# Softmax weights of a graph attention layer transposed through memory, with row sums from a 129th column

## The chip, the cores and the metric

The kernel runs on one core of a Trainium2 chip. The metric is device microseconds of that core for one execution, as the median of several runs. Engines are named as in the profile: PE (matmul) with PEld (its weight loads), DVE (vector), ACT (scalar, activations), POOL (GpSimd), SP (which issues most DMAs). Everything is float32.

## The reference

64 graphs of 256 nodes with 128 features go through four layers, each of the form x = x + layer(relu(layernorm(x))). The layers share one 256x256 adjacency matrix. What matters here is layer 0, an additive attention:

```python
W1, W2 = (W[:, :F], W[:, F:])                 # W is adj
s1 = jnp.einsum('bkf,ef->bke', x, W1)
s2 = jnp.einsum('bkf,ef->bke', x, W2)
pre = s1[:, :, None, :] + s2[:, None, :, :] + b_lin
h = jnp.where(pre >= 0, pre, ALPHA * pre)
e = jnp.einsum('bije,e->bij', h, a) + bias     # bias is adj
attn = jax.nn.softmax(e, axis=2)
out = jax.nn.sigmoid(jnp.einsum('bij,bjf->bif', attn, x))
```

For every pair of nodes of a graph 256 values are made, rectified and summed with weights: that is nearly all of the work. Layer 1 is a second message-passing layer, layer 2 a masked dot-product attention, layer 3 a gated recurrent unit of five steps.

## The kernel before

**Groups and order.** The 64 graphs go in 34 groups: two of one graph, thirty of two, two of one (`GROUPS`, line 15). No scheduler orders the instructions: the kernel writes them out in the order that a planner of its own (the loop from line 1359) finds, which keeps a clock for each engine (`Model`, line 42) with a cost for each operation, and always emits the piece of work that can start first. Pieces come from generators: `head` and `senders` prepare a graph's attention, `Pairs` makes and multiplies the pair values, `softmax0` finishes layer 0, and `layer1`, `layer2`, `layer3` or `layer3_across` follow. A `yield "pe"` in a generator names the engine that the next piece needs; a condition and an earliest time may stand behind it. Each chain of pieces has a pace (line 1322 on).

**The pairs.** A row t of a graph stands for eight tiles of 128x256 for each half (ec) of the 256 values. Three engines make such tiles: ACT (line 720, a Relu with a bias), POOL (line 725) and DVE (line 702, four or eight tiles at once). PE then sums them over the partitions with a sliding weight `a_win` (line 786); a batch is four matmuls over 512 columns (ec 0) or eight over 256 (ec 1). When at least five batches wait for PE (`SPARE`), the planner merges: DVE adds half of one batch on top of another (line 744), which costs DVE eight instructions for two rows and saves PE one batch of 256-column matmuls. So the planner trades work between DVE and PE. All `r` tiles come from 12 buffers, which PE frees.

**The end of layer 0** (`softmax0`, line 791). DVE adds the mask and takes each row's maximum (line 800); ACT takes the exponential and has its sum accumulated (line 809, an ACTIVATE and an ACTIVATION_READ_ACCUMULATOR for each half); DVE inverts the sums (line 815). PE transposes the four 128x128 blocks of weights into the PSUM bank of `e_ps` (lines 821 and 135), ACT copies them to SBUF with a factor of 0.5 (line 826), PE multiplies them with `h` (lines 832 and 128), ACT takes the tanh scaled by the inverse sums (line 839), and DVE adds the result to x (line 841).

**Transposes through memory** (`crossed`, line 97). Elsewhere 128x128 blocks are transposed by two DMAs on SP: one stores the tile to HBM (`there`, line 101), the next reads it back with its axes swapped (line 103). Both are issued one after the other, so SP waits at the read until the store has landed. The planner takes a time for the pair from a clock of its own for the memory (`TURN`, `SURE`) and lets the reader start no sooner. Groups 0 to 31 (`BY_MEMORY`) do this ahead of layers 1 and 2, groups 0 to 27 (`BY_MEMORY_3`) ahead of layer 3 and after four of its five steps.

**Layout.** h and its transpose in layer 0 are kept block by block: `h` as [128, G, 128], `h_t` as [128, G, 128], where G is the number of 128-node blocks of the group (2 or 4). In the later layers they are interleaved, [128, 128, G], so that a read of a crossing takes G neighbouring floats.

**The last two groups** and, for layer 3, groups 28 to 33 use PE transposes (`by_pe`). In `layer3` a group holds the shared PSUM banks for all five steps (`inside`, line 1262).

Of the kernel before, what the change touches and what calls it, by code (L numbers as in the profile page):

```python
# [24 lines left out]
TURN = 12500  # L25
# [16 lines left out]
class Model:  # L42
# [16 lines left out]
    def transfer(self, e):  # L59

        self.memory = max(self.memory, self.t[e] + 900) + TURN
        return self.memory + SURE
# [3 lines left out]
def kernel(ctx: ExitStack, tc: tile.TileContext, ins: dict, out: bass.AP):  # L66
# [30 lines left out]
    def crossed(src, tag, name, by, bufs=1):  # L97

        shape = [P, src.shape[1], src.shape[2]]
        there = dp.tile(shape, F32, tag="there%d" % src.shape[2], name="there", bufs=3)  # L100
        nc.sync.dma_start(out=there, in_=src)
        t = bp.tile(shape, F32, tag=tag, name=name, bufs=bufs)
        nc.sync.dma_start(out=t, in_=there.rearrange("p f g -> f p g"))
        return t, model.transfer(by)
# [67 lines left out]
    adj_n = fetch([P, 2, N], "adj_n", adj.rearrange("(c p) m -> p c m", p=P), nc.scalar)  # L172
# [66 lines left out]
    def constants0():  # L239
# [125 lines left out]
        dve(1).tensor_copy(left_b, p[:, P + 1 : P + 2])  # L365
        counts["left"] += 1
# [81 lines left out]
    def ln_relu(space, xt, tag, ln, when=None, at=None, across=False):  # L448
# [22 lines left out]
        for g in range(G):  # L471
            if g % 2 == 0:
                yield "act"
            if g == 0:
                shape = [P, P, G] if across else [P, G, P]
                h = space.tile(shape, F32, tag=ln, name=tag, bufs={ap: 3, bp: 1}.get(space))
            act(P, 2, 1).activation(  # L477
                h[:, :, g] if across else h[:, g, :], xt[:, g, :], AF.Relu, bias=shift[:, g : g + 1],
                scale=rstd[:, g : g + 1],
            )  # L480
        return h

    def transpose_blocks(space, src, name, banks, when=None, tag=None, bufs=None):

        yield "pe", when
        G, _, W = sizes(src)
        tp = banks([P, G, P], name + "_ps")
        turn()
        for g in range(G):
            tr(tp[:, g, :], src[:, g, :])  # L490
        yield "act"
        t = space.tile([P, G, P], F32, tag=tag or name, name=name, bufs=bufs)
        act(W).copy(t, tp)  # L493
        return t


    def first_head(xt, to, snd):
# [3 lines left out]
        h_t = yield from transpose_blocks(ap, h, "h0t", psum_h)  # L501
# [26 lines left out]
    def head(xt, to):  # L528
        G, _, W = sizes(xt)
        h = yield from ln_relu(ap, xt, "h0", "h0")  # L530
        h_t = yield from transpose_blocks(ap, h, "h0t", psum_h, settled)
        to.update(h=h, h_t=h_t)
        if counts["left"] > 0:
            yield from bounds(to)
# [17 lines left out]
    def bounds(of):  # L552
# [4 lines left out]
        G = h_t.shape[1]  # L557
        p = psum_h([P, P], "bound_ps")
        model.op("pe", P * 1.676)
        for c in range(G):  # L560
            nc.tensor.matmul(
                p[bass.ts(c, 32), :], lhsT=left_w, rhs=h_t[:, c, :], start=True, stop=True
            )
# [13 lines left out]
    def senders(b, of, to):  # L577

        h_t = flat(of["h_t"][:, 2 * b : 2 * b + 2, :])
        if "bound" not in of:  # L580
# [3 lines left out]
        mm(p, lhsT=left2, rhs=h_t, start=True, stop=True)  # L584
# [3 lines left out]
            adj_l, p, of["bound"][:, 2 * b : 2 * b + 1], adj_n[:, 0, :], ALU.min, ALU.add  # L588
# [6 lines left out]
        for ec in range(2):  # L595
            mm(p[:, ec, :], lhsT=w_p[:, 1, bass.ts(ec, P)], rhs=h_t, start=True, stop=True)
# [5 lines left out]
    class Pairs:  # L602
# [5 lines left out]
        def __init__(self, g, b, of, snd):  # L608
# [8 lines left out]
            self.s1n_v = of["s1n"][:, :, bass.ts(b, N)].rearrange(  # L617
                "p c (k g t) -> p c g k t", k=2, g=4
            )
            self.s1n_b = of["s1n"][:, :, bass.ts(b, N)].rearrange(  # L620
                "p c (k g t) -> p c k g t", k=2, g=4
            )
# [49 lines left out]

        def nodes(self, batch, g2):
# [3 lines left out]
                (g, k, self.b * N + 32 * g + t + (P + k if two else k * P))  # L677
# [3 lines left out]
        def make(self, who):  # L681
# [10 lines left out]
            if who == "dve":  # L692
# [4 lines left out]
                if batch["two"]:  # L697
                    s1n = self.s1n_b[:, ec, 1, 2 * g2 : 2 * g2 + n, t : t + 2].unsqueeze(3)
# [51 lines left out]
        def open(self):  # L750
            b = self.b
            self.e_ps = ps_e.tile([P, 2, N], F32, tag="e", name="e_ps")
            for ic in range(2):
                mm(
                    self.e_ps[:, ic, :], lhsT=v2_rep,
                    rhs=flat(self.of["h_t"][:, 2 * b : 2 * b + 2, :]),
# [34 lines left out]
    def softmax0(g, b, of, e_ps, snd):  # L791
# [3 lines left out]
        for ic in range(2):  # L795
            yield "dve", lambda: "adj_l" in snd

            if ic == 0:
                nmax = sp.tile([P, 2], F32, tag="nmax", name="nmax")
            dve(N, more=10).tensor_tensor_reduce(  # L800
                e_ps[:, ic, :], e_ps[:, ic, :], adj_n[:, 1, :] if ic else snd["adj_l"], -1.0, FLT_MAX,
                ALU.add, ALU.min, nmax[:, ic : ic + 1],
            )
        for ic in range(2):
            yield "act"
            if ic == 0:
                pm = ap.tile([P, 2, N], F32, tag="pm", name="pm", bufs=1)
                rs = sp.tile([P, 2], F32, tag="rs", name="rs")
            act(N, 1, more=119).activation(  # L809
                pm[:, ic, :], e_ps[:, ic, :], AF.Exp, bias=nmax[:, ic : ic + 1], scale=-1.0,  # L810
                accum_out=rs[:, ic : ic + 1],
            )
        yield "dve"
        rh = sp.tile([P, 2], F32, tag="rh", name="rh")
        dve(2).reciprocal(rh, rs)
        yield "pe"
        pt_ps = e_ps
        turn()
        for jc in range(2):
            for ic in range(2):  # L820
                tr(
                    pt_ps[:, jc, bass.ts(ic, P)], pm[:, ic, bass.ts(jc, P)]
                )
        yield "act"
        pt = ap.tile([P, 2, N], F32, tag="pt", name="pt", bufs=1)
        act(2 * N, table=1).activation(pt, pt_ps, AF.Copy, scale=0.5)
        yield "pe"
        o_ps = e_ps[:, :, 0:P]
        for ic in range(2):
            for jc in range(2):  # L830
                mm(
                    o_ps[:, ic, :], lhsT=pt[:, jc, bass.ts(ic, P)], rhs=h[:, b * 2 + jc, :],
                    start=(jc == 0), stop=(jc == 1),
                )
        for ic in range(2):
# [38 lines left out]

    def by_pe(h, tag, bufs=None, when=None, space=bp):

        yield "pe", when
        if when:
            using_a.append(tag)
        G = h.shape[2]  # L880
        tp = psum_a([P, P, G], "h_t_ps")
        turn()
        for g in range(G):
            tr(tp[:, :, g], h[:, :, g])
        yield "act"
        t = space.tile([P, P, G], F32, tag=tag, name="h_t", bufs=bufs)
        act(P * G).copy(t, tp)
        return t
# [94 lines left out]
    def layer2(x2, by_memory):  # L983
        G, NB, W = sizes(x2)
        h = yield from ln_relu(bp, x2, "h2", "h", across=True)
# [57 lines left out]
    class Home:  # L1043
# [10 lines left out]

        def bank(self, shape, name):
# [12 lines left out]
    def layer3(x3, h3, h_t, home):  # L1068
# [7 lines left out]
        for step in range(STEPS):  # L1076
            yield "pe"
# [64 lines left out]
        yield "pe"  # L1142
# [5 lines left out]
        dve(W).tensor_tensor(x3, tp.rearrange("p (g n) -> p g n", g=G), x3, ALU.add)  # L1148

    def layer3_across(x3, lane):  # L1150
# [7 lines left out]
        hn = yield from ln_relu(bp, x3, "h3" + tag, "hn" + tag, across=True)  # L1158
# [57 lines left out]
    def first_norm(g, xt):  # L1216
        h = yield from ln_relu(bp, xt, "h1", "ln", across=True)
# [4 lines left out]

    def free_a():
        return not using_a
# [5 lines left out]
    def second_rest(g, xt):  # L1230
# [6 lines left out]
        if g >= len(GROUPS) - 2:  # L1237
            hn = yield from ln_relu(rp, xt, "h3", "r", no_tiles, across=True)
            h_t = yield from by_pe(hn, "r", None, free_a, rp)
        else:  # L1240
            hn = yield from ln_relu(
                bp, xt, "h3", "hn" + tag, lambda: done3(g - 2), across=True
# [12 lines left out]
    def last_rest(g, xt, hn=None, h_t=None, home=None):  # L1255
        if home is None:
            yield from layer3_across(xt, g % 2)
        else:
            if home.banks:
                yield "pe", lambda: n == len(graphs) and not (making or doing or multiplying)  # L1260
            else:
                yield "pe", lambda: not inside
                inside.append(g % 2)
            yield from layer3(xt, hn, h_t, home)
            if not home.banks:
                inside.remove(g % 2)
# [6 lines left out]
    class Chain:  # L1273
# [14 lines left out]
        def advance(self):  # L1288

            while self.queue:  # L1290
# [8 lines left out]
                self.due = max(self.due, self.earliest)  # L1299
# [3 lines left out]
        def start(self, paced):  # L1303

            if self.engine is None or (self.when and not self.when()):
                return None
            return max(
# [16 lines left out]
    lanes = [Chain(2300), Chain(2300)]  # L1324
# [5 lines left out]
    to_load = []  # L1330
# [28 lines left out]
    while True:  # L1359
# [17 lines left out]
        for e in ("pe", "dve", "act", "pool"):  # L1377
# [28 lines left out]
            if making and (freed or not making[0].fresh()):  # L1406
                at = max(model.t[e], freed[0] if making[0].fresh() else 0.0)
                if best is None or at < best[0]:
                    best = (at, e, None)
        if best is None:  # L1410
# [61 lines left out]
```

## Time and profile before

| | us |
|---|---|
| median of three runs | 4956.28 |
| lowest and highest of them | 4955.85, 4961.90 |
| the profiled execution | 4962.75 |
| its span, first to last instruction | 4960.9 |
| first matmul of line 786 starts | 16.4 |
| last matmul of line 786 starts | 4865.7 |

The granted TensorE clock was 0.999 over the span. A busy time in the profile is the union of an engine's instruction spans. ACT's instructions overlap in its pipeline: a tile of line 720 lasts 1212 ns by the group row and the next one ends about 365 ns later. So the cost of an instruction is taken from the spacing of neighbours in the timeline, not from the mean length in the group rows. In timeline rows of PE an `xN` counts two records for a matmul instruction, except for transposes, which have one.

SP's rows are issues. DMA queue q1 carries every crossing; 204 of them are in the profile.

### The profile page before, as it was taken

To read this page: it belongs to the slowest core of one execution; us is meant where nothing else is said; L and a number is where in the kernel's file an instruction comes from. 1 tells how busy PE (TensorE), PEld (TensorE's weight loads), DVE (VectorE), ACT (ScalarE), POOL (GpSimd) and SP (SyncE) were. 2 spreads that over 40 slices of the span, in tenths; PEclk is the share of its full clock that TensorE was granted. 3 is DMA by queue.
4 is the path that set the end of the run, shared out by engine and by line. 5 is a ranking of instruction groups with operands and counts; after the bars stand their busy time and mean duration, and the time that the engine had idled before them with its cause. 6 is when DMAs were issued, how large, how long until landed. Compare 5 with 4: busy or idle time off the path is not lost.

```text
span 4960.9 us, 176723 instructions
## 1 busy us (share of the span) xinstructions
PE 4923.5 (99%) x69735; PEld 2389.7 (48%) x69735; DVE 4841.8 (98%) x8229; ACT 4873.2 (98%) x12812; POOL 4756.8 (96%) x10545
## 2 busy tenths in 40 slices
PE   9999999999999999999999999999999999999998
PEld 4454545554454544444445444444454444444444
DVE  9999999999999999999999999999999999999994
ACT  8999999999999999999999999999999999999994
POOL 8999999999999999999999999999999999999981
PEclk9999999999999999999999999999999999999999
DMA  0357576777676776866757656656666555542310
GB/s 21 10 17 23 25 30 27 32 32 30 30 33 27 32 32 28 34 27 30 33 27 30 30 27 32 32 26 32 30 32 32 26 31 30 29 26 12 19 9 8
DMA packets 3431090, 132.92 MB, mean 27 GB/s; under 512 B 3369201, under 2 KB 3405937, under 8 KB 3430257
## 3 DMA queue, kind: packets, MB, share of 16 engines
q1 hardware_dynamic: 3429712, 121.35, 56.5%
q8 instruction: 547, 8.96, 0.9%
q14 instruction: 287, 2.34, 0.3%
q10 hardware_dynamic: 544, 0.26, 0.0%
HBM read 61.48 MB, written 60.10 MB: 25 GB/s over the span
## 4 chain that ended last, share of the span: by engine, by line
PE 85%; ACT 7%; DVE 5%; POOL 1%; issue 1%; DMA 0%; ACTq 0%; DVEq 0%; POOLq 0%
PE e_ps L786 53%; PE gate_ps L128 8%; PE hv_ps L128 5%; ACT r L720 5%; PE m_ps L128 5%; PE s_ps L128 3%; DVE r L702 3%; PE o_ps L128 2%; PE e_ps L128 2%; PE rc_ps L128 1%; POOL r L725 1%; PE rsum_ps L128 1%; DVE r L744 1%; PE e_ps L135 1%; PE th_ps L128 1%
## 5 line engine op out<-in xcount | busy, mean ns | idle before, releaser
L725 POOL TENSOR_SCALAR r<-s,s1n 128x256 f32<-128x256 f32 x9920 | 4509.6, 543 | 47.1 <-PE e_ps L786 21.1
L720 ACT ACTIVATE r<-s_act,s 128x256 f32<-128x256 f32 x9768 | 4421.0, 1212 | 1.1 <-PE e_ps L786 1.0
L786 PE MATMUL e_ps<-r,a_win 128*32 128x256 f32 (+1 forms) x41040 | 3323.2, 464 | 9.1 <-DVE r L702 7.5
L702 DVE TENSOR_TENSOR r<-s_ps,s1n 128x2048 f32<-128x2048 f32 (+1 forms) x1367 | 2417.3, 1804 | 0.0
L786 PEld LDWEIGHTS e_ps<-r,a_win 128*32 128x32 f32 x41040 | 1394.2, 110 | 1603.7 <-issue 825.0
L744 DVE SCALAR_TENSOR_TENSOR r<-s_ps,s1n,r 128x256 f32<-128x256 f32 x4056 | 1671.5, 472 | 0.8 <-POOL r L725 0.3
L477 ACT ACTIVATE h<-xt,bsh,brs 128x128 f32<-128x128 f32 x512 | 417.6, 1318 | 7.5 <-POOL bsh L470 7.5
L720 ACT ACTIVATE r<-s,s 128x256 f32<-128x256 f32 x512 | 319.2, 1416 | 0.0
L128 PE MATMUL m_ps<-adj_q,hn 128*32 128x256 f32 x4096 | 252.1, 380 | 1.6 <-ACT hn L1140 1.6
L128 PEld LDWEIGHTS m_ps<-adj_q,hn 128*32 128x32 f32 x4096 | 160.8, 132 | 89.4 <-issue 25.4
L1192 ACT ACTIVATE gate_ps<-gate_ps,bz 128x512 f32<-128x512 f32 (+1 forms) x140 | 202.5, 1447 | 0.0
L1194 ACT ACTIVATE hv_ps<-hv_ps,bh 128x512 f32<-128x512 f32 (+1 forms) x140 | 200.9, 1435 | 0.0
L1180 ACT ACTIVATE m_ps<-gate_ps,br 128x512 f32<-128x512 f32 (+1 forms) x140 | 194.0, 1386 | 0.0
L1176 ACT COPY m_t<-m_ps 128x512 f32<-128x512 f32 (+1 forms) x140 | 184.7, 1319 | 0.0
L128 PE MATMUL gate_ps<-m_t,t_w_w 128*32 128x512 f32 (+1 forms) x1360 | 174.8, 568 | 0.4 <-ACT m_t L1090 0.3
L128 PE MATMUL hv_ps<-rh,u_th 128*32 128x512 f32 (+1 forms) x1360 | 170.9, 567 | 1.3 <-DVE rh L1103 1.3
L128 PE MATMUL gate_ps<-m_t,w_t 128*32 128x512 f32 (+1 forms) x1360 | 171.1, 568 | 0.6 <-ACT m_ps L1100 0.6
L128 PE MATMUL hv_ps<-m_t,t_w_w 128*32 128x512 f32 (+1 forms) x1360 | 171.0, 567 | 0.0
L809 ACT ACTIVATE pm<-e_ps,nmax 128x256 f32<-128x256 f32 x128 | 145.7, 1138 | 2.4 <-DVE nmax L800 2.4
L128 PE MATMUL gate_ps<-hf,u_t 128*32 128x512 f32 (+1 forms) x1088 | 139.8, 567 | 0.0
L128 PE MATMUL s_ps<-h0t,w_p 128*32 128x256 f32 (+1 forms) x1568 | 138.9, 445 | 0.6 <-ACT h0t L493 0.5
L940 ACT ACTIVATE th_ps<-th_ps,a_src 128x256 f32<-128x256 f32 x128 | 134.8, 1053 | 1.5 <-PE th_ps L128 1.5
(223 smaller groups left out, 4612.8 us busy)
## 6 DMA issues: line engine op xcount, KB each, us to landing
there<-hf SPq DMA_DIRECT2D x104, 256.0 KB
hn<-there SPq DMA_DIRECT2D x104, 256.0 KB
there<-h SPq DMA_DIRECT2D x86, 256.0 KB
h_t<-there SPq DMA_DIRECT2D x60, 256.0 KB
xt<-in_x_dram SPq DMA_DIRECT2D x30, 256.0 KB
out_dram<-xt SPq DMA_DIRECT2D x30, 256.0 KB
h3t<-there SPq DMA_DIRECT2D x26, 256.0 KB
row<-rows SPq DMA_DIRECT2D x128, 0.5 KB
```

The costliest lines, as they stand in the source:

```text
L128: nc.tensor.matmul(out[bass.ts(c, 32)], lhsT=lhsT[:, bass.ts(c, 32)], rhs=rhs, **flags)
L477: act(P, 2, 1).activation(h[:, :, g] if across else h[:, g, :], xt[:, g, :], AF.Relu, bias=shift[:, g : g + 1], scale=rstd[:, g : g + 1],)
L702: nc.vector.tensor_tensor(r[:, 2 * g2 : 2 * g2 + n, :, :], s2[:, ec : ec + 1, :].unsqueeze(1).to_broadcast([P, n, 2, N]), s1n.to_broadcast ...
L720: nc.scalar.activation(r[:, g, ic, :], s2[:, ec, :], AF.Relu, bias=s1[:, ec, i : i + 1])
L725: nc.gpsimd.tensor_scalar(r[:, g, ic, :], s2[:, ec, :], FLT_MAX, s1n[:, ec, i : i + 1], ALU.min, ALU.max,)
L744: nc.vector.scalar_tensor_tensor(r[:, g, ic, :], self.own("dve")[:, 1, :], self.of["s1n"][:, 1, i : i + 1], r[:, g, ic, :], ALU.max, ALU.add,)
L786: nc.tensor.matmul(to, lhsT=a_win[:, sign, 31 - t : 63 - t], rhs=of, start=False, stop=self.over, skip_group_check=True,)
L809: act(N, 1, more=119).activation(pm[:, ic, :], e_ps[:, ic, :], AF.Exp, bias=nmax[:, ic : ic + 1], scale=-1.0, accum_out=rs[:, ic : ic + 1],)
L1176: act(W).copy(m_t, m_ps)
L1180: act(W, 1).activation(m_ps, g_ps, AF.Tanh, bias=br, scale=0.5)
L1192: act(W, 1).activation(g_ps, g_ps, AF.Tanh, bias=bz, scale=0.5)
L1194: act(W, 1).activation(hv_ps, hv_ps, AF.Tanh, bias=bh)
```

## The change

In layer 0 the softmax weights of groups 0 to 31 (62 graphs) go through `crossed`; the last two graphs keep the PE transposes. The exponential no longer accumulates its sum. `h` of layer 0 gets a 129th column that holds 2.0 (written by POOL), so the product with the weights gives twice the row sum beside the output; DVE inverts that from PSUM after the product. `h` itself stays block by block, seen through a swapped view; its transpose `h_t`, and with it everything ordered by node in layer 0 (`s1`, `s1n`, `s2`, the columns of `e_ps`, the mask `adj_j`), becomes interleaved.

`crossed` now issues the store at once and puts the read in a list; the planner issues it when its clocks have passed the time at which the store should have landed. The memory clock is split in a store part and a read part. In `layer3` a group takes the shared banks for one step at a time, and the pace of the layer-3 lanes goes from 2300 to 1700 ns.

```diff
-TURN = 12500
+STORE = 1300
+LANDED = 2700
+FETCH = 10300
 SURE = 7000
...
-        self.memory = max(self.memory, self.t[e] + 900) + TURN
+        self.memory = max(self.memory, self.t[e] + 900) + STORE
+        return self.memory + LANDED - STORE
+    def fetch(self, landed):
+        self.memory = max(self.memory, landed) + FETCH
         return self.memory + SURE
...
-    def crossed(src, tag, name, by, bufs=1):
+    def crossed(src, tag, name, by, bufs=1, space=bp):
-        shape = [P, src.shape[1], src.shape[2]]
+        shape = [P, P, src.shape[2]]
         there = dp.tile(shape, F32, tag="there%d" % src.shape[2], name="there", bufs=3)
-        nc.sync.dma_start(out=there, in_=src)
-        t = bp.tile(shape, F32, tag=tag, name=name, bufs=bufs)
-        nc.sync.dma_start(out=t, in_=there.rearrange("p f g -> f p g"))
-        return t, model.transfer(by)
+        nc.sync.dma_start(out=there, in_=src[:, 0:P, :])
+        t = space.tile(shape, F32, tag=tag, name=name, bufs=bufs)
+        due = [None]
+        landed = model.transfer(by)
+        def read():
+            nc.sync.dma_start(out=t, in_=there.rearrange("p f g -> f p g"))
+            due[0] = model.fetch(landed)
+        reads.append((landed, read))
+        return t, due
...
+                if space is ap:
+                    plain = space.tile([P, G, P + 1], F32, tag=ln, name=tag, bufs=3)
+                    h = plain.rearrange("p g f -> p f g")
...
+        if space is ap:
+            pool(80).memset(h[:, P : P + 1, :], 2.0)
...
-        h_t = flat(of["h_t"][:, 2 * b : 2 * b + 2, :])
+        h_t = of["h_t"][:, :, 2 * b : 2 * b + 2]
...
-        mm(p, lhsT=left2, rhs=h_t, start=True, stop=True)
+        mm(pairs(p), lhsT=left2, rhs=h_t, start=True, stop=True)
...
                 mm(
-                    self.e_ps[:, ic, :], lhsT=v2_rep,
-                    rhs=flat(self.of["h_t"][:, 2 * b : 2 * b + 2, :]),
+                    pairs(self.e_ps[:, ic, :]), lhsT=v2_rep,
+                    rhs=self.of["h_t"][:, :, 2 * b : 2 * b + 2],
...
-                pm = ap.tile([P, 2, N], F32, tag="pm", name="pm", bufs=1)
-                rs = sp.tile([P, 2], F32, tag="rs", name="rs")
-            act(N, 1, more=119).activation(
-                pm[:, ic, :], e_ps[:, ic, :], AF.Exp, bias=nmax[:, ic : ic + 1], scale=-1.0,
-                accum_out=rs[:, ic : ic + 1],
-            )
-        yield "dve"
-        rh = sp.tile([P, 2], F32, tag="rh", name="rh")
-        dve(2).reciprocal(rh, rs)
-        yield "pe"
-        pt_ps = e_ps
-        turn()
-        for jc in range(2):
-            for ic in range(2):
-                tr(
-                    pt_ps[:, jc, bass.ts(ic, P)], pm[:, ic, bass.ts(jc, P)]
-                )
-        yield "act"
-        pt = ap.tile([P, 2, N], F32, tag="pt", name="pt", bufs=1)
-        act(2 * N, table=1).activation(pt, pt_ps, AF.Copy, scale=0.5)
-        yield "pe"
-        o_ps = e_ps[:, :, 0:P]
+                pm = ap.tile([P, P, 2, 2], F32, tag="pm", name="pm", bufs=1)
+            act(N, 1).activation(
+                pm[:, :, :, ic], pairs(e_ps[:, ic, :]), AF.Exp, bias=nmax[:, ic : ic + 1],
+                scale=-1.0,
+            )
+        src = pm.rearrange("p q j i -> p q (j i)")
+        if g in BY_MEMORY:
+            pt, at = crossed(src, "pt", "pt", "act", 1, ap)
+            yield "pe", None, at
+        else:
...
+        o_ps = e_ps[:, :, 0 : P + 1]
         for ic in range(2):
             for jc in range(2):
                 mm(
-                    o_ps[:, ic, :], lhsT=pt[:, jc, bass.ts(ic, P)], rhs=h[:, b * 2 + jc, :],
+                    o_ps[:, ic, :], lhsT=pt[:, :, 2 * jc + ic], rhs=h[:, :, b * 2 + jc],
                     start=(jc == 0), stop=(jc == 1),
                 )
+        yield "dve"
+        rh = sp.tile([P, 2], F32, tag="rh", name="rh")
+        dve(2, more=120).reciprocal(rh, o_ps[:, :, P])
+        o_ps = o_ps[:, :, 0:P]
...
-    lanes = [Chain(2300), Chain(2300)]
+    lanes = [Chain(1700), Chain(1700)]
...
+        if reads and (best is None or best[0] >= reads[0][0]):
+            reads.pop(0)[1]()
+            continue
```

## The prediction

> **What bounds the kernel now.** I read the page's busy times first, then the chain of work that ended last, then the waits.
>
> ```profile
> PE 4923.5 (99%) x69735; PEld 2389.7 (48%) x69735; DVE 4841.8 (98%) x8229; ACT 4873.2 (98%) x12812; POOL 4756.8 (96%) x10545
> ...
> PE 85%; ACT 7%; DVE 5%; POOL 1%; issue 1%; DMA 0%; ACTq 0%; DVEq 0%; POOLq 0%
> ```
>
> All four engines look full, and a busy PE need not be PE at its peak, so the spacing of instructions has to tell. PE's timeline in a steady stretch (start, length, engine, line, operation):
>
> ```profile
> 2015.88 1.05 PE L128 MATMUL e_ps<-h0t,v_rep 128*32 128x256 f32 x16
> 2016.74 1.04 PE L786 MATMUL e_ps<-r,a_win 128*32 128x512 f32 x8
> ...
> 2027.96 1.04 PE L128 MATMUL gate_ps<-m_t,t_w_w 128*32 128x512 f32 x8
> 2028.93 0.66 PE L135 MATMUL e_ps<-ident,pm 128*128 128x128 f32 x4
> 2029.51 2.79 PE L786 MATMUL e_ps<-r,a_win 128*32 128x512 f32 x32
> ...
> 2125.57 1.12 PE L128 MATMUL s_ps<-g_t,h_t 128*32 128x256 f32 x16
> 2126.50 5.35 PE L786 MATMUL e_ps<-r,a_win 128*32 128x512 f32 x64
> ```
>
> From start to start, eight matmuls of 256 columns (x16) take 0.86 us, so 0.107 each. If every PE instruction between the first and the last pair matmul cost what its kind costs in such undisturbed places, PE would need 4791 us for that stretch; it took 4849 (16.4 to 4865.7). So PE works there at 98.8% of its own floor: **PE is the bound**. The other three have no slack to speak of either: ACT's tiles follow every 0.365 us in 28 tiles of one run, POOL's every 0.453 in 64. The kernel is balanced, and what matters is the smallest saving among the engines, PE's above all.
>
> After the last pair matmul things differ:
>
> ```profile
> 4866.00:4961.00 95.00, 77.71 (x1106) 38.60 (x1098) 36.66 (x88) 39.83 (x94) 4.49 (x14) 0.96 0.03 7
> ```
>
> In these last 95 us (busy PE, PEld, DVE, ACT, POOL) PE is busy for 77.7, and by undisturbed costs for 72: the tail has some 17 to 23 us of idle PE.
>
> **The change, part by part.** Counts come from the two built programs; the clock is full in the steady part.
>
> *PE.* (1) 62 graphs lose four transposes. In the rows above the x8 run before them would take 0.86, and it takes 0.97 and then 0.58 passes to the next start: 1.55 - 0.86 = 0.69, say 0.70 us a graph, 43.4 us in all. (2) The planner sees a freer PE and merges less: 3760 instructions of line 744 instead of 4056, for which PE gets 296 more 256-column matmuls: 296 x 0.107 = +31.7 us. (3) `h_t` is now read two floats out of four. The nearest row is `s_ps<-g_t,h_t`, whose moving operand is read so: 0.93 for its two products, against 0.86 for `e_ps<-h0t,v_rep`, contiguous. Over all such rows it is +0.025 to 0.03 per product. Five products a graph (two for `e_ps`, two for `s2`, one for `left`) in 60 graphs: 300 x 0.027 = +8.1 us. The planner doesn't know this cost. Bounds: 0, if the strided weights in that row are to blame, and 10; I take 8. (4) The 129th column and the transposes of layer 0 into strided PSUM: the 129-column product takes 0.887 where the 128-column one takes 0.875, so +0.8 us; for the transposes 0 to 4, I take 2. Strided weights in `pt` cost nothing: `o_ps<-wm,elu_m`, strided, and `e_ps<-h,pt`, contiguous, both take 0.218 a product. Sum: -43.4 + 31.7 + 8.1 + 0.8 + 2 = **-0.8 us**. The saving on PE has been spent on less merging and on the layout.
>
> *The other engines.* DVE: 296 merges x 0.392 = -116.0; half instructions of line 702 +60 x 1.131 = +67.9; whole ones +8 x 2.198 = +17.6; 64 inversions of line 815 (0.072) become ones from PSUM, which after line 1035 take from 0.077, and the planner sets 0.12 more: 0 to +8, taken 5. Sum -25 us. ACT: 62 copies of line 826 x 0.488 = -30.3, 128 accumulator reads x 0.091 = -11.6, 60 more tiles x 0.365 = +21.9: -20 us. POOL: 68 tiles fewer x 0.453 = -30.8, 34 small memsets x 0.045 = +1.5: -29 us. The exponential that writes every other float I take at its old cost: `h` of line 477 is written every fourth float for 384 of its 512 instructions, and its spacing is 0.38 for most of both kinds.
>
> *The end.* In the new order 659 PE instructions stand behind the last pair matmul instead of 575: all of group 31's layer 3 (five steps, not four) and group 32's layer 2. That is 5 products of 512 columns (4.3 us), 7 of 256 (3.0), 6 of 128 or 129 (1.3) and three groups of transposes, 11 us with the strides. So the last pair matmul comes 0.8 + 11.2 = 12 us earlier. The tail grows by something between 0, if the 11 us fit into the idle 17 to 23, and 11. The last group's own chain of steps ends the tail, and PE is nearly full there until about 4947; I take +6.
>
> *Waits of PE.* PE lost 58 us against its floor. The others save 20 to 29 us where PE's stretch shortens by 12, so their tiles are ready earlier: 0 to -17, I take -5.
>
> *Memory and SP.* 62 stores and 62 reads of 256 KB are added. One crossing before:
>
> ```profile
> 2047.62 0.33 SPq L101 DMA_DIRECT2D there<-hf  x1
> 2049.69 0.36 SPq L103 DMA_DIRECT2D hn<-there  x1
> ...
> 2078.38 5.26 SPq L101 DMA_DIRECT2D there<-h  x1
> 2085.51 0.36 SPq L103 DMA_DIRECT2D h_t<-there  x1
> 2085.91 9.85 SPq L149 DMA_DIRECT2D xt<-in_x_dram  x1
> ```
>
> The read is issued 2.07 us after the store; its 16,384 packets of 16 bytes take 9.8 us from first to last in the packet records (8.6 to 10.3), the store's 128 packets 0.8. Whatever stands behind a read waits in SP for its packets (9.85 in the last row). Two graphs take 151 us; seven crossings of 10.6 us fill 74 us of it, nine will fill 95, or 63%. The consumer of the read issued at 2049.69 starts at
>
> ```profile
> 2071.78 1.91 PE L128 MATMUL m_ps<-adj_q,hn 128*32 128x256 f32 x32
> ```
>
> which is 22.1 us later; packets start 0.6 after the issue, so some 11 us are slack, and the waits list no PE idle time ended by a DMA. The planner keeps the same margin (7 us) and now counts 11.6 us a crossing where 10.6 are needed. So I cost the memory at nothing. What hides it is that slack; gone, every microsecond of a late read is PE's, because the product with `pt`, which waits, stands ahead of the pair matmuls in PE's queue. The pm stores also wait for ACT on SP, and behind them stand other groups' stores and reads.
>
> [...]
>
> *Sum.* -12 (last pair matmul) + 6 (tail) - 5 (waits) = **-11 us**, on the profiled execution's 4962.75. That one lies 6.5 us above the median of the runs and just above the highest; taken to the median, 4956.3 - 11 = **4945 us**.
>
> **Rivals.**
> *PE is not what counts.* If the 58 us that PE lost are mostly waits for tiles, the saving of the other three comes through: -20 to -29 on each, so about -25: 4931. For it: ACT and POOL have no gaps at all. Against: PE's idle time ahead of line 786 is 9.1 us in the page, and gaps above the longest regular start distance sum to 20 us between 100 and 4850.
>
> *Nothing is left.* The 11 us that move behind the last pair matmul come back in full, and the waits stay: -0.8, and with both ends of the stride price -9 to +3: about 4956. For it: PE is nearly full in the tail's first 80 us.
>
> *Reads come late: slower.* Place: the read of `pt`, and the reads of `hn` and `h_t` queued with it. A read now stands behind whatever stores SP was given meanwhile, and a store waits for its source:
>
> ```profile
> SPq L101 <- DVE hf L1202: 1367.4, 67, 31.8
> SPq L101 <- ACT r L720: 733.9, 60, 79.5
> ```
>
> (sum in us, times, longest). In this case the change doesn't do what it says: the read isn't issued when its write has landed but when the store ahead of it is ready. Price: slack is about 11 us; one more read ahead of it (9.8) uses nearly all, a second makes 9 us late. It decides from 11 / 62 = 0.18 us of PE wait per graph; at 0.5 us per graph it costs 31, so -11 + 31 = +20: 4976. Against: the built order puts one or two stores between a landing and its read, and most sources are emitted before that.
>
> **How the numbers follow.** A difference under 0.2% (9.9 us) can hardly be told from no change here. Small gain with PE as the bound: 0.60, between -20 and +2, so 0.36 faster and 0.24 same. Full savings: 0.10, faster. Nothing left: 0.12, same (0.01 of it faster). Late reads: 0.18, slower. Together faster 0.47, same 0.35, slower 0.18. The range must hold 8 in 10: from 4928, below the full savings, to 4974, which takes in the smaller half of the late reads. The small gain's own range is 4936 to 4958.
>
> **What would show it.** Right: PE at 99% with 296 more matmuls of line 786's kind; the strided products of `h_t` at 0.46 instead of 0.43; the last pair matmul near 4854 on a like execution; no PE wait on a DMA; q1's share up by a quarter to a third. Wrong: PE idle ahead of the product with `pt`, or of `m_ps`, ended by `there`; SP waits at a store with landed reads behind it; a tail longer than 106 us; or DVE, ACT and POOL still gapless and PE with fewer gaps, which is the full saving.

## The result, and the profile after

| | before | after |
|---|---|---|
| median of 20 runs each, us | 4955.94 | 4963.79 |
| lowest to highest | 4953.95 to 4961.90 | 4960.90 to 4965.82 |
| the profiled execution | 4962.75 | 4962.28 |

The ratio of after to before is 1.0016, 95% interval 1.0010 to 1.0022: **7.9 us slower**, where 11 us less had been forecast. Before runs at two levels, near 4956 and near 4962, whose profiled executions differ in the pace of POOL; the one profiled first was on the upper level, so after is set beside a second profiled execution of before (below: *e1*), at the pace of POOL that after had.

| us | e1 (before again) | after | difference | forecast |
|---|---|---|---|---|
| first to last pair matmul | 4842.3 | 4829.6 | -12.7 | -17 |
| last pair matmul to the end of the span | 95.5 | 114.2 | **+18.8** | +6 |
| sum | | | +6.1 | -11 |

So the main stretch did much of what was forecast. The tail gave it all back and more: of the 17 us between the forecast sum and the measured one, 13 are the tail's and 4 the stretch's.

The page's busy times and chain for after:

```profile
PE 4915.3 (99%) x70079; PEld 2524.1 (51%) x70079; DVE 4821.8 (97%) x8002; ACT 4854.1 (98%) x12682; POOL 4707.9 (95%) x10511
...
PE 90%; DVE 6%; ACT 4%; issue 1%; DMA 0%; POOL 0%; DVEq 0%; ACTq 0%; POOLq 0%
```

PE is at 99% again, the other three a little lower than before, and the chain runs over PE for 90% of the span instead of 85%. None of this tells of a loss. PE's timeline of after, in the steady part (start, length, engine, line, operation; line 820 is what 786 was, 591 is the bound of layer 0, one product for each block of `h_t`):

```profile
2017.57 1.10 PE L142 MATMUL e_ps<-h_t,v_rep 128*32 128x256 f32 x16
2018.48 1.05 PE L820 MATMUL e_ps<-r,a_win 128*32 128x512 f32 x8
...
2096.96 0.64 PE L591 MATMUL bound_ps<-h_t,left_w 128*32 128x128 f32 x8
2097.40 1.11 PE L142 MATMUL e_ps<-h_t,v_rep 128*32 128x256 f32 x16
```

The bound in before:

```profile
2101.76 0.40 PE L561 MATMUL bound_ps<-h0t,left_w 128*32 128x128 f32 x8
2101.97 3.63 PE L786 MATMUL e_ps<-r,a_win 128*32 128x256 f32 x56
```

From start to start, the two products of `h_t` take 0.91 where the contiguous ones took 0.86: the price of pairs of floats, as forecast. The bound takes 0.44; before, and again in a kernel below (*e10*), it takes 0.22. It now reads one float out of four. The forecast had no term for it.

The tail of after (window, its length, then busy PE, PEld, DVE, ACT, POOL, each with its instructions; the granted clock; DMA share; GB/s):

```profile
4846.00:4960.00 114.00, 90.38 (x1266) 44.58 (x1258) 41.94 (x104) 47.46 (x108) 6.94 (x23) 0.95 0.02 6
```

Against the 95.00 with 77.71 busy shown for before, PE is busy 12.7 us longer, and idle for 23.6 instead of 17.3. So the work that moved behind the last pair matmul was not taken up by idle PE; idle PE grew. Rows of PE's timeline in that tail, where brackets give the idle time before a row, if any, and what ended it:

```profile
4851.44 1.12 PE L142 MATMUL e_ps<-h,pt 128*32 128x129 f32 x32 [0.68 <-ACT pt L858]
...
4854.55 0.64 PE L142 MATMUL g_ps<-h_t,qk 128*32 128x256 f32 x8 [0.69 <-ACT h_t L520]
...
4862.13 1.09 PE L142 MATMUL o_ps<-hv,pm 128*32 128x129 f32 x32
...
4865.74 0.50 PE L149 MATMUL h_t_ps<-ident,h 128*128 128x128 f32 x2
...
4936.18 1.07 PE L142 MATMUL m_ps<-adj_q,hn 128*32 128x256 f32 x16 [0.46 <-ACT hn L1173]
...
4945.22 0.48 PE L149 MATMUL y_ps<-ident,hf 128*128 128x128 f32 x2 [1.68 <-DVE hf L1163]
4947.10 0.67 PE L149 MATMUL hn_ps<-ident,hf 128*128 128x128 f32 x2 [1.41 <-DVE hf L1163]
4948.24 1.94 PE L142 MATMUL m_ps<-adj_q,hn 128*32 128x256 f32 x16 [0.46 <-ACT hn L1173]
...
4956.20 0.67 PE L149 MATMUL y_ps<-ident,hf 128*128 128x128 f32 x2 [2.06 <-DVE hf L1163]
```

The like rows of before: the last product with `pt` (group 33), the transposes that begin its layer 1, and the ends of layer 3 of groups 32 and 33.

```profile
4870.52 1.06 PE L128 MATMUL e_ps<-h,pt 128*32 128x128 f32 x32
...
4876.18 0.51 PE L135 MATMUL h_t_ps<-ident,h 128*128 128x128 f32 x2
...
4952.35 0.51 PE L135 MATMUL y_ps<-ident,hf 128*128 128x128 f32 x2
...
4957.25 0.48 PE L135 MATMUL y_ps<-ident,hf 128*128 128x128 f32 x2 [1.68 <-DVE hf L1130]
```

In after, group 33, the last, has its product with `pt` at 4851.4. By the kernel's condition `free_a`, its layer 1 can begin (the transposes at 4865.74) only when group 32's layer 2 (4854.55 to 4862.13) has let go of the PSUM bank that both use: 14.3 us, where before it was 5.7 (4870.5 to 4876.2). Group 33 ends its five steps of layer 3 at 4945.22; then group 32 still has its last one, from 4947.10 on, alone, each operation waiting for the one ahead. Before, group 33 ended last. Counted from the last pair matmul, group 33 ends 7.7 us later than in before (99.2 for 91.5), and the step that group 32 still does takes 11.0 more: together nearly all of the tail's growth.

Of the memory, the waits of SP (sum in us, times, longest):

```profile
SPq L108 <- ACT r L754: 879.7, 86, 71.7
...
SPq L108 <- ACT pm L842: 115.3, 8, 54.2
SPq L114 <- DMA there<-pm: 87.1, 44, 4.3
```

Stores do wait on SP for their source, as the rival said. But the waits list names no wait of PE for a DMA. The product with `pt` starts 4.0 to 11.7 us (median 8.4) after the packets of its read have ended. One late read shows: the read of one `pt`, the third in a row on SP, was issued 11.9 us after its store, the bank of `e_ps` that waited for it came free late, and PE waited 3.1 us at 1930, once. Queue q1 carries 74.0% instead of 56.5%.

### The profile page after: what moved, and what is told of

It reads as the page before. It is cut to its first block, busy times and chain, and to the rows that moved or that the text cites. A ratio compares the mean times of both kernels' runs of the same rounds, so it can differ in the third digit from the quotient of the medians.

```text
span 4960.3 us, 177317 instructions
## 1 busy us (share of the span) xinstructions
PE 4915.3 (99%) x70079; PEld 2524.1 (51%) x70079; DVE 4821.8 (97%) x8002; ACT 4854.1 (98%) x12682; POOL 4707.9 (95%) x10511
## 4 chain that ended last, share of the span: by engine, by line
PE 90%; DVE 6%; ACT 4%; issue 1%; DMA 0%; POOL 0%; DVEq 0%; ACTq 0%; POOLq 0%
PE e_ps L820 57%; PE gate_ps L142 8%; PE hv_ps L142 6%; PE m_ps L142 5%; DVE r L736 3%; PE s_ps L142 3%; ACT r L754 3%; PE e_ps L142 2%; PE o_ps L142 2%; PE rc_ps L142 2%; PE rsum_ps L142 1%; DVE r L778 1%; PE left_ps L142 1%; PE y_ps L142 1%; PE th_ps L142 1%
## 5 line engine op out<-in xcount | busy, mean ns | idle before, releaser
L754 ACT ACTIVATE r<-s_act,s 128x256 f32<-128x256 f32 x9828 | 4137.5, 916 | 8.8 <-PE e_ps L820 8.3
L736 DVE TENSOR_TENSOR r<-s_ps,s1n 128x2048 f32<-128x2048 f32 (+1 forms) x1435 | 2502.3, 1785 | 4.8 <-PE e_ps L820 4.7
L820 PEld LDWEIGHTS e_ps<-r,a_win 128*32 128x32 f32 x41632 | 1506.6, 110 | 1529.0 <-issue 806.7
L778 DVE SCALAR_TENSOR_TENSOR r<-s_ps,s1n,r 128x256 f32<-128x256 f32 x3760 | 1549.3, 475 | 0.5 <-ACT r L754 0.2
L500 ACT ACTIVATE h<-xt,bsh,brs 128x128 f32<-128x128 f32 x512 | 319.3, 908 | 11.2 <-POOL bsh L490 8.2
L1228 ACT ACTIVATE gate_ps<-gate_ps,bz 128x512 f32<-128x512 f32 (+1 forms) x140 | 143.4, 1024 | 0.0
L142 PE MATMUL s_ps<-h_t,w_p 128*32 128x256 f32 (+1 forms) x1568 | 141.8, 452 | 0.8 <-ACT h_t L520 0.5
L1230 ACT ACTIVATE hv_ps<-hv_ps,bh 128x512 f32<-128x512 f32 (+1 forms) x140 | 142.3, 1017 | 0.0
L1216 ACT ACTIVATE m_ps<-gate_ps,br 128x512 f32<-128x512 f32 (+1 forms) x140 | 133.7, 955 | 1.3 <-PE gate_ps L142 0.6
L488 POOL TENSOR_TENSOR brs<-bve,neg_half 128x4 f32<-128x4 f32 (+1 forms) x136 | 133.7, 983 | 0.0
```

Source lines behind the costliest of these rows:

```text
L142: nc.tensor.matmul(out[bass.ts(c, 32)], lhsT=lhsT[:, bass.ts(c, 32)], rhs=rhs, **flags)
L488: pool(1085).tensor_tensor(rstd, ve, neg_half[:, 0:G], ALU.pow)
L500: act(P, 2, 1).activation(h[:, 0:P, g], xt[:, g, :], AF.Relu, bias=shift[:, g : g + 1], scale=rstd[:, g : g + 1],)
L736: nc.vector.tensor_tensor(r[:, 2 * g2 : 2 * g2 + n, :, :], s2[:, ec : ec + 1, :].unsqueeze(1).to_broadcast([P, n, 2, N]), s1n.to_broadcast ...
L754: nc.scalar.activation(r[:, g, ic, :], s2[:, ec, :], AF.Relu, bias=s1[:, ec, i : i + 1])
L778: nc.vector.scalar_tensor_tensor(r[:, g, ic, :], self.own("dve")[:, 1, :], self.of["s1n"][:, 1, i : i + 1], r[:, g, ic, :], ALU.max, ALU.add,)
```

## The experiments

All of these compute the whole reference. Each was timed beside runs of before on its own chip. In this table the stretch is from the start of the first to that of the last pair matmul, the tail from there to the end of the span, and POOL the mean spacing of its undisturbed tiles; these three come from one profiled execution, the ratio and its 95% interval from the timed runs.

| | median, us | ratio to before | stretch | tail | POOL, ns |
|---|---|---|---|---|---|
| before, first profile | | | 4849.3 | 95.2 | 453.7 |
| e1 before again | (one run: 4956.32) | | 4842.3 | 95.5 | 451.7 |
| after, first profile | 4963.79 | 1.0016 (1.0010 to 1.0022) | 4829.6 | 114.2 | 451.7 |
| e9 after again | 4971.66 | 1.0016 (1.0007 to 1.0025) | 4834.3 | 114.4 | 454.0 |
| e5 banks held for five steps | 4960.54 | 0.9996 (0.9987 to 1.0005) | 4844.3 | 95.6 | 454.1 |
| e6 before, banks shared by steps | 4967.16 | 1.0011 (1.0002 to 1.0019) | 4833.8 | 114.0 | 454.0 |
| e2 four graphs more by PE | 4969.31 | 1.0014 (1.0005 to 1.0023) | 4835.6 | 114.9 | 454.0 |
| e8 late reads alone | 4962.22 | 0.9999 (0.9990 to 1.0008) | 4846.8 | 97.5 | 454.0 |
| e3 no weights through memory | 4998.18 | 1.0072 (1.0059 to 1.0084) | 4849.1 | 126.5 | 451.7 |
| e7 contiguous layout | 4970.78 | 1.0015 (1.0007 to 1.0024) | 4848.4 | 103.0 | 454.0 |
| e10 the same, other exponential | 4956.92 | 0.9989 (0.9980 to 0.9998) | 4836.9 | 100.0 | 453.5 |
| e11 planner told the costs | 4966.96 | 1.0009 (1.0000 to 1.0018) | 4847.1 | 99.7 | 453.6 |

The theory after the result: the sharing of the banks step by step in layer 3, a small part of the change, lengthens the tail by what it saves ahead of it and more. The rivals: the latency of the crossing delays the last groups; reads issued late delay others; the strides cost more than counted.

**e1, before again**, no edit and one run: is the first profile of before a fair partner?

> The kernel before, unchanged, for a second profile, because its first profiled execution (4962.75 us) lies 6.5 above the median of its runs (4956). If that one was ordinary, this one has its last pair matmul near 4866 and a tail of 95 us again. If it was an odd one, time is near 4956 and the trace shows where the 7 us were: in the tail (88 us, the clock drop around 4880 to 4900 gone) or in the main stretch (last pair matmul near 4859).

Its tail is the same (95.5), its stretch 7.0 us shorter. POOL's tiles follow every 451.7 ns instead of 453.7, ACT's every 364.4 instead of 365.1, DVE's every 391.8 in both. The 7 us go with that pace and not with anything in the tail. **e9, after again**, no edit either, shows the same for the changed kernel: tail 114.4, stretch 4.7 us longer with POOL at 454.0, and a ratio to before on that chip of 1.0016 once more.

> The changed kernel once more, beside the others on the same chip, so that they are compared at one level of POOL's and ACT's spacing. Theory: last pair matmul between 4829 and 4838 after the first, by POOL's spacing (451.7 or 454 ns), tail 112 to 116, ratio to before 1.000 to 1.002.

**e5, the change without the sharing.** A group that holds the banks keeps them to the end of its five steps:

```diff
         def free(self):
-            return self.banks or not inside
+            return self.banks or self in inside or not inside
...
-            if not self.banks:
+            if not self.banks and self not in inside:
                 inside.append(self)
...
-            home.leave()
```

> The changed kernel with one part undone: in layer 3 a group on the shared banks keeps them for all five steps again. Theory tail: the last pair matmul stays near 4846, the work behind it falls from 658 PE instructions to 576 and the tail from 114 us to about 95, time 4944 to 4950, faster than before by 0.1 to 0.25%. Theory memory: the crossing's latency holds up groups 31 and 32, so the tail stays above 105 us and time is 4957 to 4964. Theory layout (strided reads of the transpose cost PE): the last pair matmul moves to 4856 or later.

The tail falls from 114.4 (e9) to 95.6 at the same pace of POOL, the stretch grows by 10.0 (the expectation had forgotten that the moved work then comes back ahead of the last pair matmul), and the ratio goes from 1.0016 to 0.9996. So the sharing costs the changed kernel 9 to 10 us. Without it the change is even with before.

**e6, the sharing alone, in before**: `free`, `enter` and `leave` of the changed layer 3 in the kernel before, nothing else.

```diff
-            yield "pe"
+            yield "pe", home.free
+            home.enter()
...
-            else:
-                yield "pe", lambda: not inside
-                inside.append(g % 2)
```

> The kernel before with that one part alone: layer 3 on the shared banks takes them for one step at a time. Theory tail: 654 PE instructions stand behind the last pair matmul instead of 574, the tail grows from 95 to 105 to 114 us, the main stretch shortens by some 10, time 4959 to 4967. Theories memory and layout: this part is harmless, time within 3 us of 4956.

```profile
4850.50:4965.00 114.50, 90.29 (x1266) 44.76 (x1258) 42.06 (x104) 47.25 (x110) 6.99 (x23) 0.95 0.02 6
```

This is the tail of e6, to be read beside the one of after above: nearly the same length, work of PE and idle time, without one softmax weight sent through memory. Here too group 33's layer 1 begins late (16.2 us after its product with `pt`), and group 32's last step runs alone at the end. The stretch is 15.5 us shorter than in before's first profile, but 4.3 of this are 40 pair matmuls that the planner merged away in the new order. The tail is 18.8 longer, and the ratio says slower. So the cause of the longer tail is shown from both sides. The new pace of the layer-3 lanes was not run by itself; e5 has it and e6 has not, and the tail follows the sharing in both.

**e2, the last groups by PE.** If the crossing's latency made the tail, groups 30 and 31 on PE would shorten it.

```diff
-        if g in BY_MEMORY:
+        if g < 30:
             pt, at = crossed(src, "pt", "pt", "act", 1, ap)
```

> The changed kernel, but groups 30 and 31 (four graphs) transpose their softmax weights on PE as before; all else as changed. Theory (sharing of the banks lengthens the tail): no difference, tail 112 to 118, PE work behind the last pair matmul 83 as with the change, time within 4 us of the changed kernel. Rival (the crossing's latency of some 20 us delays the last groups and that makes the tail): tail 95 to 105, time 8 to 15 us lower.

Tail 114.9, ratio within the interval of e9. That rival falls.

**e8, the late reads alone, in before**: the changed `crossed`, `transfer` and `fetch`, with the weights transposed on PE as before.

```diff
-        nc.sync.dma_start(out=t, in_=there.rearrange("p f g -> f p g"))
-        return t, model.transfer(by)
+        reads.append((landed, read))
+        return t, due
...
+        if reads and (best is None or best[0] >= reads[0][0]):
+            reads.pop(0)[1]()
+            continue
```

> Before with the late reads alone: the store is issued at once, the read from a list when the planner's clocks have passed its landing. Nothing else is changed; softmax weights stay on PE. Theory: reads were never awaited by a consumer, so SP's waiting at a read cost nothing and undoing it gains nothing; the PE sum from the built order is +2.6 us, the tail's work 75.3 against 72.0. So 4956 to 4966 beside before's 4956 to 4963, ratio within 0.9985 to 1.0015, tail 95 to 99. Rival, the late reads are what makes the change slower (reads behind stores that wait): +6 us or more, and waits of PE ended by a DMA. Rival, they are what bought the shorter main stretch: last pair matmul 8 us or more earlier.

Even with before (the interval leaves some 5 us either way): the stretch is 2.4 us shorter than in before's first profile, the tail 2.3 longer. Issuing a read once its write has landed neither cost nor bought time that shows here.

**e3, no crossing of the weights.** All else of the change stays; every graph transposes on PE.

```diff
-        if g in BY_MEMORY:
+        if g < 0:
             pt, at = crossed(src, "pt", "pt", "act", 1, ap)
```

> The changed kernel with the softmax weights of all graphs transposed on PE again; everything else stays (interleaved layout, 129th column, late reads, layer 3 sharing its banks step by step). Theory tail (the crossing pays in the main stretch, the step-by-step sharing in layer 3 takes it back at the end): PE has 43.4 us of transposes more and 232 pair matmuls of 256 columns fewer (24.9), so the last pair matmul comes about 20 us later than in the changed kernel, the tail stays 114 us, time about 4980 to 4984. Theory memory (the crossing itself costs what is lost): the tail falls back to 95 us and time is at or below 4960.

The stretch is 19.5 us longer than in after, so the transposes that PE is spared are worth about that once the planner has traded the rest for fewer merges. Some 6 of it are the new layout: four transposes of `pm`, which now read one float out of four, take 0.68 us from start to next start (as at 2040.05), against 0.58 in before. The tail is 126.5, longer than the theory gave. It has as many PE instructions as after's (1266 records in the windows of both) in another order. The granted clock was halved in it in four stretches of 3.4 to 6.8 us, in after's in one of 6.8, and in both again in the last few us. Of the 12 us between the two tails, 5.6 are longer busy time of PE, which goes with the lower clock (0.89 for 0.95 in the windows), and the rest is more idle PE. Why the idle time grew was not settled.

**e7, the layout undone.** `h_t` contiguous again and no node order interleaved, banks held for five steps, pace 1500; the exponential does the reordering, writing every fourth float.

```diff
+            act(N, 1).activation(
+                pm[:, :, :, ic].rearrange("p q j -> p j q"),
+                e_ps[:, ic, :].rearrange("p (j q) -> p j q", j=2), AF.Exp,
```

> The crossing of the softmax weights, the 129th column and the late reads are kept. Undone are the interleaved layout (h_t, the node order of s1, s2, e_ps, adj_j; the exponential alone reorders, by reading e_ps as written and writing pm strided) and the sharing of the banks step by step (layer 3 holds them for five steps); the layer-3 pace is 1500 ns. Theory: the strided moving operands cost PE about 7 us at the pair-strided products (300 x 0.024) and 7 at the bound (0.439 against 0.218), and the tail was 19 longer through the sharing alone. Then left is at 0.43, the bound at 0.22, the tail at 95 to 98, and with 24 more merges than e5 (12648 pair matmuls of 256 columns by line and order against 12632, but a PE floor of 4855.7 against 4854.0 + 14 for strides) the time is 8 to 13 us under that of e5: 4947 to 4953, below before. Rival, ACT and POOL are the bound now (their gaps were already few): PE's 12 us turn into idle time, time within 3 us of e5, 4957 to 4963, and PE's gaps ahead of the pair matmuls grow by 8 or more. Rival, a strided exponential costs ACT: exponential spaced more than 0.1 us wider.

A miss. PE's prices fell as expected: 0.43 for `left`, 0.22 for the bound. But the stretch is 4 us longer than in e5 where it should have been about 12 shorter, and the exponential took ACT 0.661 us (its end less the end of the instruction before, median of 108), against 0.404 in after and 0.366 in before. 128 of them at 0.26 more are 33 us of ACT that the planner didn't count.

**e10, the same order of instructions, another exponential**: it reads PSUM in jumps of 512 bytes and writes every other float, as in after.

```diff
-                pm[:, :, :, ic].rearrange("p q j -> p j q"),
-                e_ps[:, ic, :].rearrange("p (j q) -> p j q", j=2), AF.Exp,
+                pm[:, :, :, ic], e_ps[:, ic, :].rearrange("p (j q) -> p q j", j=2), AF.Exp,
```

> As e7_contiguous, the same instructions in the same order, except that the exponential reads e_ps with jumps of 512 bytes (alternating halves) and writes every other float of pm, where in e7 it read straight and wrote every fourth float. In e7 it is spaced 0.661 us, with the change 0.404, before 0.366 (366 without the accumulator read). Theory: e7 lost because ACT, with 124 times 0.26 = 32 us more than the planner counted, became what PE waits for; its strides on PE did go (left 0.43, bound 0.22). If the stride of the write is the price (stride two +0.04, stride four +0.29), the exponential falls to 0.40 to 0.42, ACT loses its 32 us and the time comes to what the PE sum promised, 4948 to 4957 beside before's 4956 to 4963: 12 to 22 under e7's standing. Rival, any reordering in the exponential costs this much: 0.6 or more and e7's time, ratio 1.0005 to 1.0025. Rival, ACT was not what held e7: the exponential falls and the time stays within 4 us of e7's standing.

ACT's timeline of e7 first, then of e10, around the two exponentials of one graph:

```profile
2024.60 2.88 ACT L735 ACTIVATE r<-s_act,s 128x256 f32<-128x256 f32 x6
2026.75 1.41 ACT L823 ACTIVATE pm<-e_ps,nmax 128x256 f32<-128x256 f32 x1
2027.31 2.89 ACT L735 ACTIVATE r<-s_act,s 128x256 f32<-128x256 f32 x6
```

```profile
2021.79 2.51 ACT L735 ACTIVATE r<-s_act,s 128x256 f32<-128x256 f32 x5
2023.58 1.12 ACT L823 ACTIVATE pm<-e_ps,nmax 128x256 f32<-128x256 f32 x1
2023.95 2.91 ACT L735 ACTIVATE r<-s_act,s 128x256 f32<-128x256 f32 x6
```

The tiles ahead of it end at 2027.48 in e7 and at 2024.30 in e10 (start plus length), the exponential at 2028.16 and 2024.70: 0.68 and 0.40. Only this differs in the two kernels, and the ratio falls by 0.0026, some 13 us. In the profiles 11.5 of them are in the stretch and 2.9 in the tail, where e7 had the clock halved for a longer time (granted clock 0.93 in its window, 0.97 in e10's). The jumps in PSUM cost nothing (0.40, as in after, which reads in order), the stride of the write does. e10 is the fastest kernel here: ratio 0.9989 (0.9980 to 0.9998), some 5 us under before.

**e11, the planner told.** e5 with the strides in the planner's costs, pace 1500.

```diff
-        model.op("pe", max(n, 64) * 1.676)
+        model.op("pe", max(n, 64) * 1.676 + (24 if len(rhs.shape) == 3 and rhs.shape[2] == 2 else 0))
...
-        model.op("pe", P * 1.676)
+        model.op("pe", 439)
...
-            act(N, 1).activation(
+            act(N, 1, more=38).activation(
```

> As e5_hold (the change with layer 3 holding the banks for five steps), but the planner is told the costs that the traces showed: 24 ns more for a product with a pair-strided moving operand, 439 for the bound where it counted 215, 38 more for the exponential; layer-3 pace 1500 ns. It then merges more: 120 fewer pair matmuls of 256 columns than e5 by line and order (12512 against 12632), PE's floor 12.9 us lower, work behind the last pair matmul 73.2 against 72.5. Theory: PE at its floor is the bound and its strides are a cost the planner can trade if it knows them: 5 to 13 us under e5, ratio to before 0.997 to 0.9985, last pair matmul 5 to 13 us earlier than e5's 4861.6 at the same POOL spacing, tail 95 to 99. Rival, the merges that are added go to a DVE without slack (30 halves of merges more at 0.392 for each eight, 120 / 8 x 8 x 0.392 = 47 us on DVE, less the rows it gives up): no gain, within 3 us of e5, and DVE gapless ahead of its merges.

A miss for the theory: PE's floor went down by 12.9 us and the stretch up by 2.8; PE's idle time between 100 and 4840 sums to 14.6 us, against 9.5 in e5. Here a saving on PE that was bought with DVE time did not come through (the pace differs from e5's too, 1500 for 1700, and was not run by itself). Which of the other engines PE then waits for was not settled; DVE made 120 more merges (3872 instructions at line 778, against 3752) and 41 row instructions fewer (1403 at line 736, against 1444).

## Why the prediction was wrong

**The step that failed is "The end": "I take +6", between 0 and 11.** The prediction counted the work that moves (11 us; by the built orders 83.0 against 72.0 us of PE) and set it against idle PE (17 to 23 us), as if a tail were a stretch with a bound engine. The tail is the end of chains, and measured +18.8, 8 above the upper bound. In the windows shown PE is busy 12.7 us longer, and its idle time, into which the work was to fit, did not shrink but grew by 6.3 us, because group 32's layer 2 holds the bank that group 33's layer 1 wants, and group 32's last step of layer 3 is left to run alone. The list of signs named a tail over 106 us as the mark of an error, and so it was. The cause was in the diff, "a group takes the shared banks for one step at a time"; the prediction priced its effect on the count and not on the order of the last groups. e6 shows the effect without the rest of the change, and e5 shows the rest without the effect.

**The rest of the sum, in its own terms.**
- PE's four transposes against 296 more matmuls: -11.7 forecast. The trace of after has the counts (248 transposes fewer and 592 records of pair matmuls more than e1, two records each). Right.
- Strided `h_t`: 300 products at 0.027, +8.1. Measured 0.024, +7.3. Right.
- The bound at line 591 was left out: 30 groups at 0.22, **+6.6 us**. It reads `h_t` too, and every reader of a moved layout has to be listed. Strided transposes into PSUM: 2 forecast, nothing measured (four of them take 0.586 us to the next start, 0.587 before). PE's sum is then +3.0 and not -0.8.
- The exponential "at its old cost": measured 0.404 for 0.366, 128 x 0.038 = +4.9 us of ACT. The row it was argued from (`h` with and without stride, 0.38 both) was no sign that the stride is free: its 128 floats take longer than the 256 of a tile (0.365), so something other than the writing of floats seems to set its spacing. e7, where a stride of four costs 0.29, shows how large this could have been.
- The last pair matmul: -12 forecast from PE alone, -8 with PE's sum at +3.0 and 11 us of moved work. The 4.7 us that are left to the -12.7 measured would be fewer waits (5 forecast); this is a remainder and not a measurement.
- Memory at nothing: right. Nine crossings in place of seven, no PE wait for a DMA, one stall of 3.1 us. The rival of the late reads had the sign that came, but did not happen: e8 is even, and the loss lies in the tail. The row of 9.8 us for a read held: the 62 reads of `pt` in after take 8.6 to 10.4 us from first to last packet, median 9.8. With 124 transfers more the mean DMA share lies between 0.71 and 0.96 over stretches of 500 us from 500 to 4500 (0.49 to 0.73 in before), and one stall of PE is all that came of it.

**PE as the bound** stands only in part. 33 us more of ACT cost some 13 us (e7 against e10), a POOL slower by 0.5%, with ACT slower by 0.2%, goes with 5 to 7 us (e1, e9), and 13 us less of PE for more of DVE bought nothing (e11). The kernel has no single bound, and by these sizes a sum for PE alone can be off by some 10 us, which is the size of what was to be forecast.

## What to carry to other kernels

Price the last groups by following their chain to the end, bank by bank; a count of work set against idle time was no bound for the tail here (at most 11 us counted, 18.8 measured). When a layout moves, list every reader and writer of it on every engine, with the stride that each then has. And in a balanced kernel take two profiles of the kernel before: here the two lie 6.4 us apart (4962.75 and 4956.32), where the change was worth 7.9.

## What the runs showed of the hardware

- **Strides.** For 256 floats written by ACT: contiguous 0.366 us, every other float 0.404, every fourth 0.661 (128 exponentials in each kernel). For a moving operand of PE: two floats of four +0.024 on 0.432, one of four 0.439 for 0.218 (four column groups, 128 columns each), and four transposes that read one of four 0.68 for 0.58 (e3). In PSUM no price showed: ACT's reads in jumps of 512 bytes leave the exponential at 0.40 (e10; in after, which reads in order, 0.404), and four transposes into strided PSUM take 0.586 where they took 0.587.
- **Two paces.** POOL's tiles followed every 451.7 ns in three profiled executions and every 453.5 to 454.1 in nine; ACT's every 364.4 and 365.1 to 365.3 in the same ones; DVE's always every 391.7 to 391.8. It goes with 5 to 7 us of the stretch, evenly over the graphs. What sets it was not found.
- **The clock in the tail.** In the tails the granted clock was halved for 3.4 to 6.8 us at a time: in the row of after at 4948.24, 16 records take 1.94 us at a clock of 0.50, where the like row at 4936.18 takes 1.07 at 1.00. In the tails of all twelve profiles PE was busy for 14 to 49% of the 3.4 us just before each halving (not every stretch as idle was followed by one); what sets it off was not shown. Group 32's last step in after had both: waits of 0.46 to 2.06 us ahead of four of its rows, and a clock of 0.50 from 4948 to 4952.
